# Adding the gather's z half from PSUM by VectorE, a full-height PSUM fill and a reordered last stage in a fused two-layer graph kernel

## The chip, the cores and the metric

One core of one Trainium2 chip. The metric is the device time of one launch in microseconds (us), the median of several runs. Executions of one kernel agree here to 0.1 to 0.2%. Ratios are formed only of kernels that ran in the same rounds on the same chip; where two experiments of different rounds are set side by side, the kernel before, which ran in all of them, differed by at most 0.6 us between the sets.

## The reference, cut to what matters

```python
# x (64, 256, 512), adj (64, 256, 256), nodemask all ones; float32
def layer0(x, adj, W):
    deg = sum(adj, -1)
    agg = adj @ x / max(deg, 1e-6)
    return relu(concat([x, agg], -1) @ W.T)          # 512 outputs
x = layernorm(x + layer0(x, adj, W))
def layer1(X, adj, mask, Wqk, Wv):
    q, k = split(X @ Wqk);  v = X @ Wv
    w = mask * rowsum(q * (adj @ (k * mask))) / sqrt(512)
    return softmax(w, axis=nodes)[..., None] * v
x = layernorm(x + layer1(x, adj, mask, Wqk, Wv))
```

The 64 graphs are worked on as 32 pairs, and layer 1 of one pair is interleaved with layer 0 of the next.

## The kernel before

All large products are done by a fast scheme with seven products in place of eight (named P1 to P7), some of them split once more. So the kernel is made of many matmuls of 256 or 512 columns into eight PSUM banks, with sums of blocks before and after them. TensorE runs without pause when everything is in time, and each bank is reused a few matmuls after it is read.

The part that the change is about is the product with adj of layer 0, the gather. Its bank `u` collects a running total over four steps (u1, u2, u3, u4), and after each step something reads it before the next step adds on:

```python
def gather(a, w, dst, u, p5, p2, own=None, rdeg=None, later=()):
    ...
        r12, r22 = dst[:, :, 0], dst[:, :, 1]              # the tile z, when own is given
    def onto(t, ps):                                       # own += bank * rdeg, first half of the columns
        for k in range(2):
            r = own[:, k, t, :HF]
            vec.scalar_tensor_tensor(r, ps[:, k * HF:(k + 1) * HF], rdeg[:, k, t:t + 1], r,
                                     op0=OP.mult, op1=OP.add)
    def u2():
        twice(u, "S2", "T2", start=False)
        act.copy(r12, of(u))                               # z from PSUM by ScalarE
        ...
    def u3():
        twice(u, "S3", "T3", start=False)
        act.copy(r22, of(u))
        vec.tensor_add(r22, of(p5), r22)
    def g3():
        twice(p5, "S4", "B22", start=False)
        vec.tensor_add(r12, of(p5), r12)
    def u4():
        twice(u, "A22", "T4", start=False)
        ...
# later, in norm0: own[second half] += z * rdeg, four VectorE instructions for a pair
```

VectorE, ScalarE, GpSimd and the DMA queue each have one queue, filled in the order in which the program issues to them. That order comes from a small model in the kernel: chains of steps (`queue`) are drained at `tick`, when the model thinks that an engine is free.

```python
def tick():
    while not quiet[0]:
        for c in list(chains):
            if c[2][0] <= clock[0] and c[3][0][0].free <= clock[0] + room[c[3][0][0]]:
                step(c)
                break
        else:
            return
```

The final scaling of layer 1 on ScalarE, with the output transfer behind it, is the chain "finish"; whatever is left of it is flushed where the next pair begins, ahead of the load of adj:

```python
for j in range(NP):
    ...
    flush("finish")                  # scale on ScalarE, then issue out
    ...
    if j > 0:
        load_adj(j)                  # 0.5 MB, issued behind the outputs
        sumsA[j] = adj_sums(j)       # sa: sums of adj's blocks on GpSimd
```

A split product is four steps; the third waits for ScalarE's copy of the second, since it overwrites that half bank:

```python
def second():
    mm(lo, s(1), b["T2"])
    act.copy(q[0][:, HF:], lo)
def third():
    mm(lo, s(2), b["T3"])
    ...
```

And the sums of x1's transposed blocks for layer 1 (`x1T_s` on VectorE, the first row's and S1's second-level sums `x1T_i` on GpSimd) run during the gather:

```python
queue(1, "sums", *outer_sums(Y, vec), (vec, lambda Y=Y: inner_sums(Y, gp, 1)))
```

## Time and profile before

| what | before |
|---|---|
| time, median of 3 runs | 1880.53 us (1880.49 to 1882.17) |
| TensorE busy | 1859.2 us, 99% |
| VectorE busy | 1511.1 us, 80% |
| ScalarE busy | 1309.1 us, 70% |
| TensorE stalls, whole span | 26.3 us |

The last row isn't on a page of the profile. I took each matmul's start from the trace, subtracted the start of the one before, and took off the time that the columns of the one before need at full pace (0.21 us for 256 columns of f32 or 512 of bf16, 0.43 us for 512 of f32); what is over 0.04 us counts as a stall. A product that runs at half pace at the start thus counts with half its time. All stalls in this document are computed so, from one profiled execution of each kernel.

Groups of instructions are shown by tile; the columns are count, then minimum, median and maximum in ns, first and last start, shapes.

```profile
L90 DVE TENSOR_TENSOR x1T_s<-x1T_s,x1T x32: 691/692/694, 89.1 to 1841.3; 128x512 f32<-128x512 f32 x32
```

```profile
L90 DVE TENSOR_TENSOR v<-v,fifth x62: 424/426/1017, 119.3 to 1835.1; 128x256 f32<-128x256 f32 x62
```

The addition to v is 0.43 us in most pairs and over 1 us at worst.

### The profile page before, as it was taken

The page shows a single profiled execution, that of the slowest core. Times are in us where ns is not written, and L with a number is a line of the kernel's source. Part 1 is how long each engine was busy: PE and PEld are TensorE (multiplying, and loading weights), DVE is VectorE, ACT ScalarE, POOL GpSimd, SP SyncE. Part 2 cuts the span into 40 slices and gives each one's busy share as a digit, 9 for nine tenths or more (in the row PEclk, how much of TensorE's full clock was granted, in tenths as well). Part 3 has the DMA queues.
Part 4 walks back from the last instruction along what each step waited for, and adds up shares of the span by engine and source line. Part 5 has one row for each costly group of instructions (what it writes and reads, how often), then busy time and mean ns, then how long its engine had stood idle before and what let it go on. Part 6 is the DMA issues. An engine that isn't in the chain of part 4 may idle for free.

```text
span 1878.8 us, 25005 instructions
## 1 busy us (share of the span) xinstructions
PE 1859.2 (99%) x7000; PEld 1314.0 (70%) x7000; DVE 1511.1 (80%) x3180; ACT 1309.1 (70%) x3274; POOL 909.2 (48%) x1251
## 2 busy tenths in 40 slices
PE   9999999999999999999999999999999999999997
PEld 5667777767777677677677777776776777776765
DVE  6787888778887778887778887788877788877887
ACT  3667776677777677767777766777676777767766
POOL 4455443555444554535554535554445544355532
PEclk9999999999999999999999999999999999999999
DMA  6123334333333433343333334333434233433321
GB/s 225 57 69 82 100 94 113 90 90 96 107 97 88 114 82 99 90 118 85 100 91 103 96 98 106 85 99 96 110 85 113 80 103 94 110 94 86 99 64 51
DMA packets 380714, 181.27 MB, mean 96 GB/s; under 512 B 263712, under 2 KB 345248, under 8 KB 380576
## 3 DMA queue, kind: packets, MB, share of 16 engines
q1 hardware_dynamic: 380576, 179.67, 35.4%
q8 instruction: 57, 0.93, 0.2%
q14 instruction: 81, 0.66, 0.1%
HBM read 114.10 MB, written 34.06 MB: 79 GB/s over the span
## 4 chain that ended last, share of the span: by engine, by line
PE 96%; DVE 2%; ACT 1%; DMA 0%; issue 0%; POOL 0%; DVEq 0%; ACTq 0%
PE bank L175 96%; ACT own L90 1%; DVE v L90 0%; DVE own L90 0%; ACT bank L90 0%; DVE turn L90 0%; DMA wqk<-wqk_t 0%; DVE tv L90 0%; DVE y L90 0%; PE bank L628 0%; POOL xT_s L90 0%; DVE bank L90 0%; POOL sa L90 0%; ACT x1T L90 0%; DVE st L90 0%
## 5 line engine op out<-in xcount | busy, mean ns | idle before, releaser
L90 ACT COPY bank<-bank 128x256 f32<-128x256 f32 (+1 forms) x768 | 332.3, 435 | 235.8 <-PE bank L175 224.7
L90 DVE TENSOR_TENSOR y<-bank,y 128x512 f32<-128x512 f32 x256 | 170.5, 686 | 131.9 <-ACT y L90 131.3
L90 ACT ACTIVATE own<-own,shift,rstd 128x512 f32<-128x512 f32 x255 | 199.8, 808 | 0.9 <-DVE shift L90 0.9
L175 PE MATMUL bank<-tv,sa 128*128 128x256 f32 x768 | 192.5, 380 | 1.0 <-DVE tv L90 0.9
L90 POOL TENSOR_TENSOR x1T_s<-x1T,x1T_s 128x256 f32<-128x256 f32 x64 | 63.6, 1013 | 267.7 <-PE bank L175 267.7
L90 POOL TENSOR_TENSOR x1T_i<-x1T_s 128x128 f32<-128x128 f32 x128 | 101.1, 790 | 182.8 <-DVE x1T_s L90 182.8
L90 ACT ACTIVATE junk<-own,less 128x512 bf16<-128x512 f32 x254 | 183.7, 723 | 3.0 <-DVE less L90 2.1
L175 PEld LDWEIGHTS bank<-tv,sa 128*128 128x128 f32 x768 | 145.4, 190 | 49.9 <-issue 23.1
L90 ACT COPY y<-bank 128x512 f32<-128x512 f32 x192 | 108.8, 583 | 95.2 <-PE bank L175 93.7
L90 POOL TENSOR_TENSOR sa<-adj 128x256 f32<-128x256 f32 x128 | 94.7, 740 | 165.9 <-DMA adj<-adj_t 152.1
L175 PE MATMUL bank<-w,x1T_s 128*128 128x512 f32 (+1 forms) x384 | 168.3, 521 | 0.0
L90 POOL TENSOR_TENSOR x1T_i<-x1T 128x256 f32<-128x256 f32 x64 | 55.4, 866 | 221.6 <-DMA x1T<-turn 209.0
L175 PE MATMUL bank<-t,xT_s 128*128 128x512 f32 (+1 forms) x384 | 159.3, 524 | 2.5 <-ACT own L90 1.5
L175 PE MATMUL bank<-t,x1T_s 128*128 128x512 f32 (+1 forms) x384 | 158.1, 521 | 0.3 <-ACT y L90 0.3
L90 DVE TENSOR_TENSOR v<-bank,v 128x512 f32<-128x512 f32 x186 | 119.2, 682 | 48.8 <-PE bank L175 48.8
L175 PE MATMUL bank<-w,xT_s 128*128 128x512 f32 (+1 forms) x384 | 153.1, 521 | 0.0
L175 PE MATMUL bank<-t_i,xT_i 128*128 128x256 f32 x512 | 152.7, 380 | 0.3 <-DVE own L90 0.2
L175 PE MATMUL bank<-t_i,x1T_i 128*128 128x256 f32 x512 | 152.2, 379 | 0.1
L175 PEld LDWEIGHTS bank<-t_i,x1T_i 128*128 128x128 f32 x512 | 97.1, 190 | 67.1 <-issue 48.6
L175 PEld LDWEIGHTS bank<-t_i,xT_i 128*128 128x128 f32 x512 | 94.6, 189 | 58.2 <-issue 45.7
L90 ACT COPY own<-bank 128x512 f32<-128x512 f32 x128 | 71.8, 587 | 89.9 <-PE bank L175 49.3
L175 PE MATMUL bank<-t,x1T 128*128 128x512 f32 x256 | 130.4, 592 | 0.0
(159 smaller groups left out, 4565.6 us busy)
## 6 DMA issues: line engine op xcount, KB each, us to landing
x<-x SPq DMA_DIRECT2D x64, 512.0 KB, 5.7
xT<-x_t SPq DMA_DIRECT2D x62, 512.0 KB, 5.5
out<-own SPq DMA_DIRECT2D x62, 512.0 KB, 3.2
x1T<-turn SPq DMA_DIRECT2D x480, 64.0 KB, 2.3
adj<-adj_t SPq DMA_DIRECT2D x64, 256.0 KB, 3.8
turn<-adj SPq DMA_DIRECT2D x64, 256.0 KB, 3.0
row<-d SPq DMA_DIRECT2D x31, 256.0 KB, 4.7
wqk<-wqk_t SPq DMA_DIRECT2D x4, 512.0 KB, 5.7
```

The costliest lines, as they stand in the source:

```text
L90: return self.tc.keep_in_program_order(getattr(self.engine, name)(out, *args, **kwargs))
L175: tc.keep_in_program_order(nc.tensor.matmul(ps, a, b, start=start, stop=True, skip_group_check=True))
```

## The change

The intent: z disappears as a tile. VectorE adds every block of the gather straight from PSUM to x1's buffer, `own`. The rest is small: the banks are filled at the start by ten products of full height (128 rows) instead of eight of one row, the first second-level sums are split so that the start can go earlier, GpSimd's sums of S1 are queued earlier, one transposition in the last pair goes earlier, and the last pair's order becomes "p p r p r p".

```diff
-        def onto(t, ps):
+        def onto(t, h, ps):
             for k in range(2):
-                r = own[:, k, t, :HF]
+                r = own[:, k, t, h * HF:(h + 1) * HF]
@@ u2, u3, g3 (u1, g2, u4 likewise)
             twice(u, "S2", "T2", start=False)
-            act.copy(r12, of(u))
+            if own is None:
+                act.copy(r12, of(u))
+            else:
+                onto(0, 1, u)
...
+                onto(1, 1, u)
+                onto(1, 1, p5)
...
+                onto(0, 1, p5)
@@ norm0
-                work += [(vec, lambda k=k, t=t: scaled(k, t)),
-                         (vec, lambda k=k, t=t, total=total: residual(k, t, total))]
+                work.append((vec, lambda k=k, t=t, total=total: residual(k, t, total)))
@@ fill
-    ones = const.tile([1, P], BF16, name="ones")
+    ones = const.tile([P, P], BF16, name="ones")
-               ones[:, None, :].to_broadcast([1, F // P, P]), start=True)
-    for pair in banks:
+               ones[:, None, :].to_broadcast([P, F // P, P]), start=True)
+    for pair in (banks[0], *banks):
@@ start and pairs
-    inner_sums(Xs[0], gp, 0)
-    inner_sums(Xs[0], gp, 1)
+    for part in (3, 1, 4):               # 3 and 4: the two halves of part 0
+        inner_sums(Xs[0], gp, part)
-            queue(1, "sums", *outer_sums(Y, vec), (vec, lambda Y=Y: inner_sums(Y, gp, 1)))
+            outer_Y = outer_sums(Y, vec)
+            queue(1, "sums", outer_Y[0], (vec, lambda Y=Y: inner_sums(Y, gp, 1)), *outer_Y[1:])
@@ last pair
+    turn_here(X, x1, 0, pf)
     run("l", l=open1)
     flush("norm", "mask")
-    turn_here(X, x1, 0, pf)
...
-    run("p p p r p r", p=p, r=r)
+    run("p p r p r p", p=p, r=r)
```

More of the change, by code (lines that the diff above doesn't have):

```diff
@@ L123, in resnorm_kernel @@
     banks = [[psum.tile([P, F], F32, name=f"bank{2 * n + k}") for k in range(2)] for n in range(4)]
-    (adjs, rows, xs, Xs, rdegs, sumsA, sumsM, owns, ys, zs, aggs, vs, x1Ts, scores, columns, rows_d, rows_w,
-     probs) = ({} for _ in range(18))
+    (adjs, rows, xs, Xs, rdegs, sumsA, sumsM, owns, ys, aggs, vs, x1Ts, scores, columns, rows_d, rows_w,
+     probs) = ({} for _ in range(17))
     clock, chains, shared, quiet = [0.0], [], [1.0], [False]
@@ L301, in inner_sums @@
         of_sum = lambda n: lambda k, e: X.s[:, k, X.slot[n]:X.slot[n] + 1, e]
-        ks, b = ((slice(0, 2), X.first_row), (slice(2, 3), of_sum(S1)), (slice(0, 1), of_sum(S4)))[part]
+        ks, b = ((slice(0, 2), X.first_row), (slice(2, 3), of_sum(S1)), (slice(0, 1), of_sum(S4)),
+                 *((slice(v, v + 1), lambda k, e, v=v: X.first_row(k, e)[:, v:v + 1]) for v in range(2)))[part]
         a11, a12, a21, a22 = (b(k, e) for k in range(2) for e in range(2))
@@ L411, in gather @@
             r11, r12, r21, r22 = (dst[:, :, t, h * HF:(h + 1) * HF] for t in range(NT) for h in range(2))
-        else:
-            r12, r22 = dst[:, :, 0], dst[:, :, 1]
-        def onto(t, ps):
+        def onto(t, h, ps):
             for k in range(2):
-                r = own[:, k, t, :HF]
+                r = own[:, k, t, h * HF:(h + 1) * HF]
                 vec.scalar_tensor_tensor(r, ps[:, k * HF:(k + 1) * HF], rdeg[:, k, t:t + 1], r,
@@ L432, in u1 @@
             else:
-                onto(0, u)
+                onto(0, 0, u)
             spare()
@@ L441, in g2 @@
             else:
-                onto(0, p2)
+                onto(0, 0, p2)
             spare()
@@ L457, in u3 @@
             twice(u, "S3", "T3", start=False)
-            act.copy(r22, of(u))
-            vec.tensor_add(r22, of(p5), r22)
+            if own is None:
+                act.copy(r22, of(u))
+                vec.tensor_add(r22, of(p5), r22)
+            else:
+                onto(1, 1, u)
+                onto(1, 1, p5)
             tick()
@@ L463, in g3 @@
             twice(p5, "S4", "B22", start=False)
-            vec.tensor_add(r12, of(p5), r12)
+            if own is None:
+                vec.tensor_add(r12, of(p5), r12)
+            else:
+                onto(0, 1, p5)
             tick()
@@ L471, in u4 @@
             else:
-                onto(1, u)
+                onto(1, 0, u)
             tick()
@@ L524, in norm0 @@
     def norm0(j):
-        own, z, rdeg = owns[j], zs.pop(j), rdegs.pop(j)
+        own = owns[j]
         x1Ts[j] = Side(pool, "x1T", S2)
         sq = []
-        def scaled(k, t):
-            o = own[:, k, t, HF:]
-            vec.scalar_tensor_tensor(o, z[:, k, t], rdeg[:, k, t:t + 1], o, op0=OP.mult, op1=OP.add)
         def residual(k, t, total):
@@ L832, in resnorm_kernel @@
             degrees(1)
-        zs[j] = pool.tile([P, 2, NT, HF], F32, name="z")
-        g = gather(sumsA.pop(j), T, zs[j], pw[1], y[1], y[0], owns[j], rdegs[j], T_late)
+        g = gather(sumsA.pop(j), T, None, pw[1], y[1], y[0], owns[j], rdegs.pop(j), T_late)
         def sums_next():
```

## The prediction

> **What bounds the kernel now.** I read the page first: the busy shares, then the chain that ended last.
>
> ```profile
> PE 1859.2 (99%) x7000; PEld 1314.0 (70%) x7000; DVE 1511.1 (80%) x3180; ACT 1309.1 (70%) x3274; POOL 909.2 (48%) x1251
> ...
> PE 96%; DVE 2%; ACT 1%; DMA 0%; issue 0%; POOL 0%; DVEq 0%; ACTq 0%
> ```
>
> TensorE is the bound, so work removed from VectorE or ScalarE is worth only the stalls of TensorE that it ends, and work that lands late before a matmul costs directly. How much there is to win: I laid the starts of the 7000 matmuls against the pace of an unstalled row (a 128x256 f32 record every 0.216 us, a 512-wide one every 0.429 us, read in the timeline). What is over that pace is about 26 us: 2.7 in the first weight products, some 8 from 21 to 100 us, 10.7 from 150 to 1796 us (0.2 in every pair, and 0.1 to 0.5 more in every second or third pair), 3 after 1820 us. After the last matmul (1867.0) 11.8 us more follow. The first look, at the start, is the timeline of TensorE and of its weight loads:
>
> ```profile
> 1.15 3.59 PE L175 MATMUL bank<-ones 1*128 1x512 bf16 x8 [1.15 <-DVE ones L90]
> 5.22 16.62 PE L175 MATMUL bank<-wqk 128*128 128x512 f32 x32 [0.47 <-DMA wqk<-wqk_t]
> ...
> 9.65 0.34 PEld L175 LDWEIGHTS bank<-wqk 128*128 128x128 f32 x1 [0.52 <-issue]
> 10.50 0.20 PEld L175 LDWEIGHTS bank<-wqk 128*128 128x128 f32 x1 [0.52 <-issue]
> 10.95 0.19 PEld L175 LDWEIGHTS bank<-wqk 128*128 128x128 f32 x1 [0.24 <-issue]
> ```
>
> Up to 10.5 us a product takes 0.85 us, after it 0.43: half clock for 5.3 us. The second look is where z costs, by tile:
>
> ```profile
> L90 DVE SCALAR_TENSOR_TENSOR own<-z,rdeg,own x128: 469/478/1023, 55.0 to 1819.2; 128x256 f32<-128x256 f32 x128
> L90 ACT COPY z<-bank x64: 574/585/586, 49.5 to 1805.8; 128x512 f32<-128x512 f32 x64
> L90 DVE TENSOR_TENSOR z<-bank,z x64: 691/692/693, 52.0 to 1808.7; 128x512 f32<-128x512 f32 x64
> ...
> L90 DVE SCALAR_TENSOR_TENSOR own<-bank,rdeg,own x192: 469/477/486, 45.9 to 1808.2; 128x256 f32<-128x256 f32 x192
> ```
>
> Third, the border between two pairs, in ScalarE's, the DMA queue's and TensorE's timelines (one pair of thirty that look alike):
>
> ```profile
> 797.01 1.50 ACT L90 ACTIVATE own<-own,shift,rstd 128x512 f32<-128x512 f32 x2
> 798.66 0.36 ACT L90 COPY bank<-bank 128x256 f32<-128x256 f32 x1 [0.15 <-PE bank L175]
> 799.95 0.36 ACT L90 COPY bank<-bank 128x256 f32<-128x256 f32 x1 [0.93 <-PE bank L175]
> ...
> 798.54 0.38 SPq L180 DMA_DIRECT2D out<-own  x1
> 799.03 1.34 SPq L180 DMA_DIRECT2D adj<-adj_t  x2
> ...
> 800.61 0.59 PE L175 MATMUL bank<-w,x1T_i 128*128 128x256 f32 x2
> ```
>
> The copy at 799.95 empties the half bank that the matmul at 800.61 overwrites; it ends 0.30 us before it. That is all the slack there is.
>
> **What the Trainium skill says.** "TensorE: Matmul & The Clock Gate", section "What's actually happening": the array starts at half clock, and a free-running window of 3.4 us of activity releases it. The trace agrees in kind: half pace to 10.5 us. It does not show whether one-row products count as activity. "SBUF — State Buffer", section "Who interferes with whom": a VectorE instruction with two SBUF inputs contends with GpSimd's reads, one with at most one SBUF input does not. The trace agrees: own<-z (two SBUF inputs) goes up to 1023 ns, own<-bank (one) never over 486. "Perfetto Trace Analysis", section "Optimizing Scalar/DVE Operations", gives VectorE a larger fixed cost on PSUM than on SBUF; here the two medians are 477 and 478 ns, so no difference shows.
>
> **The change, part by part.**
>
> z. Per pair it removes two ScalarE copies (2 x 0.585 = 1.17 us), two VectorE adds (2 x 0.692) and four scaled adds (4 x 0.604, the mean, = 77.3 us of the group over 128). It adds eight adds from PSUM of 0.436 to 0.477 us (83.8 us of the group over 192; the median). VectorE: minus 3.80, plus 3.5 to 3.8, so nothing; ScalarE: minus 1.17. None of it is on TensorE's path in the steady state: waits put down to z are 0.2 us in all. What matters is where VectorE's reads now stand, since TensorE reuses bank u. After u2 (its matmuls end at 772.61, the next on that bank starts 1.73 us later) VectorE has one sum of 0.69 ahead and then 0.87 for two reads: done at +1.56, just in time. After u3: 1.30 us to the next use, 0.2 for the result and 0.87 of reads, with two sums of 0.7 to 0.95 in the queue: 0 to 0.2 late, I say 0.05. Times 29 pairs: +1.5 us.
>
> What z's going moves. In the order of the built programs ScalarE's queue changes at the border of pairs: before, one half's final scaling stood early (778.7 and 780.2) and the other at 797.01; now both stand at the border, two before the copy of 798.66 and two between it and the copy of 799.95. Two scalings take 1.50. Then: 798.66 + 0.29 + 1.44 = 800.39 is when the second copy can start, it ends at 800.75, and a matmul starts 0.05 to 0.15 us after the copy that it waits for: 800.85 in place of 800.61. That is +0.24 us in each of 29 pairs: **+7.0 us**.
>
> The two output transfers now also stand together ahead of the next adj: it is issued after the second scaling, at about 801.0 in place of 799.03, behind 1 MB in place of 0.5, so the GpSimd sums of adj start at some 805.4 in place of 803.36. There they meet the two v additions with two SBUF inputs that lead, by turn, bank and own, to the first product of P6. Before, this collision is the one that makes the irregular stalls: 0.425 us for that addition and no stall, or 0.93 to 1.02 and a stall of 0.35 to 0.43. I count 3.8 us over 30 pairs now, 0.13 each, and expect 0.30 each: **+5 us** (from -4, if the sums come after both additions, to +12).
>
> Start. Ten full-height products (0.43 each, 1.15 to 5.4) join the weight products without the gap of 0.47, so the clock should come up at 5 to 8 us instead of 10.5: about 2.2 gained of the 2.7, less 0.2 for the longer fill. The smaller first sums on GpSimd let P1 start that early. But VectorE is 93 to 98% busy from 30 to 50 us, and there TensorE waits for it (0.90 for tv); and in the first gather its reads of z's banks stand behind those sums (up to +1). I keep **-1**.
>
> End. The transposes of the last pair fill the 0.4 us wait at 1831.5; a P4 product between P3's steps fills the 0.7 at 1862, but the last score then comes 0.43 later, so the softmax gains about 0.4. **-0.8**.
>
> Sum: +1.5 + 7.0 + 5 - 1 - 0.8 = +11.7, that is 1892. The two large terms rest on an order and on one pair's times, and all errors that I can think of (a shorter queue on ScalarE, now 1.17 us lighter) go the other way, so I take a third off: 1888.
>
> **The rivals.** (a) A small gain: start and end give 3 to 4 us and the steady state nothing, 1877. For it: VectorE's sum is even, ScalarE's falls, GpSimd is blocked less. Against it: the free 0.30 us before 800.61. (b) VectorE becomes the bound in the gather: reads behind other work stall u3 and u4 by 0.5 us each, +29 us, 1910. For it: VectorE is 80% busy and serves its queue in order; against it: the reads fit by the times above. (c) The late adj misses the v additions altogether: the 3.8 us go, and with the +7 the whole is about 1882.
>
> **Range and chances.** Rival (a) sets the low end, less a little: 1874; the upper ends of the collision term (+12) and of u3 (+5) the high one: 1902. 2% is 37.6 us. The whole sum of stalls that could be removed is 26 us, so faster by 2% is out of reach; slower by 2% takes rival (b) in full and more.
>
> **What would show it.** Right: in each pair a stall of about 0.2 us before the w,x1T_i matmul that follows two scalings and a copy on ScalarE; both output transfers next to each other, adj landing 2 us later against TensorE, the v additions near 0.8 us; wqk products at 0.43 us from before 8 us on; no z rows; own<-bank 448 times, never over 0.5 us. Wrong: those copies ending earlier, no regular stall, adj's sums clear of the v additions (then 1876 to 1882); or long waits of TensorE for own, in the gather (then over 1900).

## The result, and the profile after

| | before | after |
|---|---|---|
| time, median of 4 runs of the same rounds | 1881.35 us (1880.49 to 1882.70) | 1908.35 us (1908.26 to 1908.41) |
| ratio after / before | | 1.0143 (1.0125 to 1.0160) |
| TensorE busy | 1859.2 us | 1874.7 us |
| VectorE busy | 1511.1 us | 1499.5 us |
| ScalarE busy | 1309.1 us | 1277.5 us |

The kernel became 1.4% slower, 27 us. That is within 2%, as the prediction thought most likely, but outside its range (1874 to 1902).

The page of the changed kernel, its busy line and its chain by engine:

```profile
PE 1874.7 (98%) x7002; PEld 1306.7 (69%) x7002; DVE 1499.5 (79%) x3244; ACT 1277.5 (67%) x3210; POOL 896.9 (47%) x1255
...
PE 89%; DVE 6%; ACT 3%; issue 1%; DMA 1%; POOL 1%; SPq 0%; DVEq 0%; ACTq 0%
```

VectorE, ScalarE and GpSimd all have less to do than before, and still the chain that ends last goes through them for more of the span. So the loss is not work; it is the time at which work is done. Where TensorE stalls, from the trace (us; the number of times in brackets):

| stall, 150 to 1820 us | before | after | predicted addition | measured addition |
|---|---|---|---|---|
| third step of P3 in layer 1 (after ScalarE's copy) | 0 | 9.7 (29) | +7.0 | +9.7 |
| u4 of the gather (after VectorE's reads of u3) | 0 | 7.4 (27) | +1.5 for u2 and u3 | +7.4 |
| first product of P6 in layer 0 (after the v additions) | 4.9 (14) | 17.1 (25) | +5 | +12.2 |
| a step of P2 in layer 0 | 5.8 (29) | 5.8 (29) | 0 | 0 |
| all stalls before 150 us | 12.7 | 10.5 | -1 | -2.1 |
| all stalls after 1820 us | 3.0 | 3.2 | -0.8 | +0.3 |

In sum the stalls go from 26.3 to 54.0 us, 27.7 more, and the last matmul starts 27.8 us later (1866.99, then 1894.79). The account closes.

**u4.** VectorE's three x1T_s sums and GpSimd's first sum of them in one gather of the kernel before (start and duration in us):

```profile
772.75 0.68 DVE L90 TENSOR_TENSOR x1T_s<-x1T 128x512 f32<-128x512 f32 x1
773.47 0.69 DVE L90 TENSOR_TENSOR x1T_s<-x1T_s,x1T 128x512 f32<-128x512 f32 x1
774.08 0.94 DVE L90 TENSOR_TENSOR x1T_s<-x1T 128x512 f32<-128x512 f32 x1
...
773.51 0.96 POOL L90 TENSOR_TENSOR x1T_i<-x1T_s 128x128 f32<-128x128 f32 x1 [4.80 <-DVE x1T_s L90]
```

The three sums follow each other here, and only the third is lengthened, to 0.94 us. The timelines of VectorE, GpSimd and TensorE of the changed kernel in one gather:

```profile
374.05 0.68 DVE L90 TENSOR_TENSOR x1T_s<-x1T 128x512 f32<-128x512 f32 x1
374.65 0.87 DVE L90 SCALAR_TENSOR_TENSOR own<-bank,rdeg,own 128x256 f32<-128x256 f32 x2
375.44 0.91 DVE L90 TENSOR_TENSOR x1T_s<-x1T_s,x1T 128x512 f32<-128x512 f32 x1
376.27 0.94 DVE L90 TENSOR_TENSOR x1T_s<-x1T 128x512 f32<-128x512 f32 x1
377.13 1.65 DVE L90 SCALAR_TENSOR_TENSOR own<-bank,rdeg,own 128x256 f32<-128x256 f32 x4
...
375.76 0.90 POOL L90 TENSOR_TENSOR x1T_i<-x1T_s 128x128 f32<-128x128 f32 x1
376.62 0.90 POOL L90 TENSOR_TENSOR x1T_i<-x1T_s,x1T_i 128x128 f32<-128x128 f32 x1
...
378.05 1.13 PE L175 MATMUL bank<-tv,adj 128*128 128x256 f32 x4
```

The first `own<-bank` row is the two reads of u2. They now stand between the first and the second x1T_s sum, and this pushes the second sum into the time of GpSimd's own sums of the first (375.76 and 376.62). The second sum takes 0.91 us where it took 0.69; the third takes 0.94 as before. The reads of u3 start at 377.13; the first two of them are done near 378.0, and u4, at 378.05, waits for them.

**Third step.** ScalarE, the DMA queue and TensorE at the border of two pairs, in the changed kernel:

```profile
398.66 1.50 ACT L90 ACTIVATE own<-own,shift,rstd 128x512 f32<-128x512 f32 x2
400.32 0.36 ACT L90 COPY bank<-bank 128x256 f32<-128x256 f32 x1 [0.15 <-PE bank L175]
400.59 1.52 ACT L90 ACTIVATE own<-own,shift,rstd 128x512 f32<-128x512 f32 x2
402.01 0.37 ACT L90 COPY bank<-bank 128x256 f32<-128x256 f32 x1
...
400.19 2.32 SPq L180 DMA_DIRECT2D out<-own  x2
402.62 1.32 SPq L180 DMA_DIRECT2D adj<-adj_t  x2
...
402.52 0.67 PE L175 MATMUL bank<-w,x1T_i 128*128 128x256 f32 x2
```

Two scalings now stand between the two copies, and the second copy ends at 402.38 instead of with 0.30 us to spare. The matmul pair waits 0.255 us for it. It then shows 0.67 us where an unstalled pair shows 0.59: the second matmul loses 0.078 us more. Both outputs are issued ahead of adj.

**P6.** GpSimd, VectorE, ScalarE and TensorE later in the same pair:

```profile
406.96 0.73 POOL L90 TENSOR_TENSOR sa<-adj 128x256 f32<-128x256 f32 x1 [7.62 <-DMA adj<-adj_t]
407.76 0.80 POOL L90 TENSOR_TENSOR sa<-sa,adj 128x256 f32<-128x256 f32 x1
408.52 0.72 POOL L90 TENSOR_TENSOR sa<-adj 128x256 f32<-128x256 f32 x1
...
407.48 0.48 DVE L90 TENSOR_TENSOR v<-v,fifth 128x256 f32<-128x256 f32 x1
...
408.60 0.92 DVE L90 TENSOR_TENSOR v<-v,fifth 128x256 f32<-128x256 f32 x1
409.45 1.29 DVE L90 STREAM_TRANSPOSE turn<-own 128x512 f32<-128x512 f32 x2
410.67 1.39 DVE L90 TENSOR_TENSOR bank<-bank,fifth 128x256 f32<-128x256 f32 x4
...
411.10 1.07 ACT L90 COPY own<-bank 128x512 f32<-128x512 f32 x2 [1.63 <-DVE bank L90]
...
411.82 1.96 PE L175 MATMUL bank<-t,xT_s 128*128 128x512 f32 x4 [0.23 <-POOL sa L90]
```

adj came late, so GpSimd's sums of it reach over both additions to v: here the first takes 0.48 and the second 0.92 us, where an undisturbed one takes 0.43. The delay travels on: behind the additions VectorE has the transposition (turn) and the sums in bank, ScalarE's copies to own wait 1.63 us for those, and the first product of P6 overwrites the bank that the first of these copies reads: that copy ends at 411.68, P6 starts at 411.82. In the kernel before at most one of a pair's two additions is over 0.44 us (16 of 31 pairs); now both are in 22 of 31. The group over the whole run, by tile, moves its median from 426 to 904 ns:

```profile
L90 DVE TENSOR_TENSOR v<-v,fifth x62: 424/904/969, 117.3 to 1863.4; 128x256 f32<-128x256 f32 x62
```

The matmul's line names GpSimd's `sa` as the releaser. That is only the semaphore that came last by the profile: these sums aren't an operand of it, 18 of the 25 waits of this kind are put down to ScalarE's copy to own, and adj_early below, which takes away the collision, takes away this stall.

### The profile page after: what moved, and what is told of

Same layout as the page of the kernel before. It is cut to its first block, busy times and chain, and to the rows that moved or that the text cites. A ratio compares the mean times of both kernels' runs of the same rounds, so it can differ in the third digit from the quotient of the medians. Undisturbed runs are those within 1.5% of the kernel's fastest.

```text
span 1906.6 us, 24982 instructions
## 1 busy us (share of the span) xinstructions
PE 1874.7 (98%) x7002; PEld 1306.7 (69%) x7002; DVE 1499.5 (79%) x3244; ACT 1277.5 (67%) x3210; POOL 896.9 (47%) x1255
## 4 chain that ended last, share of the span: by engine, by line
PE 89%; DVE 6%; ACT 3%; issue 1%; DMA 1%; POOL 1%; SPq 0%; DVEq 0%; ACTq 0%
PE bank L175 89%; ACT own L90 2%; DVE v L90 2%; DVE own L90 1%; ACT bank L90 1%; DVE turn L90 1%; DMA w<-w_t 1%; DVE bank L90 0%; DVE t_i L90 0%; DVE t L90 0%; POOL xT_s L90 0%; DVE tv L90 0%; POOL sa L90 0%; DVE y L90 0%; SPq L180 0%
## 5 line engine op out<-in xcount | busy, mean ns | idle before, releaser
L90 DVE SCALAR_TENSOR_TENSOR own<-bank,rdeg,own 128x256 f32<-128x256 f32 x448 | 189.0, 472 | 12.5 <-PE bank L175 12.3
L90 POOL TENSOR_TENSOR x1T_s<-x1T,x1T_s 128x256 f32<-128x256 f32 x64 | 67.9, 1079 | 273.0 <-PE bank L175 273.0
L90 POOL TENSOR_TENSOR x1T_i<-x1T_s 128x128 f32<-128x128 f32 x128 | 88.0, 687 | 179.1 <-DVE x1T_s L90 179.1
L90 DVE TENSOR_TENSOR agg<-bank,agg 128x512 f32<-128x512 f32 x96 | 65.5, 683 | 125.9 <-ACT agg L90 124.7
```

What stands on the lines that cost most here:

```text
L90: return self.tc.keep_in_program_order(getattr(self.engine, name)(out, *args, **kwargs))
```

## The experiments

**The theory:** all three losses come from orders of queues that z's removal moved. (1) Both final scalings at the border delay ScalarE's copy: the third step. (2) adj behind two outputs lets GpSimd's sums block both v additions: P6. (3) The reads of u2 push the second x1T_s sum, too, under GpSimd's sums: u4. **Rivals:** A, the other parts of the change cost the time; B, VectorE is simply too full, or its reads from PSUM cost as such, so that moving queues gains little.

The results in one table; stalls in us from 150 to 1820 us, of one profiled run each. "u4" counts the wait before it and inside it. The profiled run isn't always a median one: that of finish_early took 1885.28 us, 1.9 below its median.

| kernel | time (us) | ratio to before | third step | u4 | P6 |
|---|---|---|---|---|---|
| before | 1881.35 | 1 | 0 | 0 | 4.9 |
| after | 1908.35 | 1.0143 | 9.7 | 7.4 | 17.1 |
| z_only | 1909.64 | 1.0148 | 9.7 | 6.7 | 15.7 |
| rest_only | 1879.35 | 0.9988 | 0 | 0 | 6.7 |
| adj_early | 1891.70 | 1.0055 | 9.7 | 7.4 | 0.2 |
| finish_early | 1887.13 | 1.0030 | 0 | 7.2 | 3.2 |
| gp_wait | 1907.37 | 1.0140 | 9.7 | 7.1 | 16.1 |
| gp_wait2 | 1899.44 | 1.0098 | 9.7 | 0 | 14.7 |
| s3_late | 1884.41 | 1.0015 | 0 | 3.1 | 5.4 |
| all3 | 1878.55 | 0.9986 | 0 | 3.0 | 0.5 |
| all4 | 1875.61 | 0.9971 | 0 | 0 | 0.6 |
| rest_adj | 1873.79 | 0.9959 | 0 | 0 | 0.3 |
| fill_only | 1879.73 | 0.9993 | 0 | 0 | 4.1 |
| row10 | 1881.92 | 1.0003 | 0 | 0 | 6.5 |

In the rows before and after the times are those of the result's own rounds. The kernel before measured 1880.94, 1881.48 and 1880.97 us in the three sets of rounds (first four experiments; gp_wait, s3_late, all3 and rest_adj; the last four). The 95% intervals of the ratios are about 0.0014 to either side. All experiments computed correct results.

**z_only.** The kernel before with only the z hunks (`gather`, `norm0`, no z tile).

> The kernel before with only the z part of the change. Theory (three losses by order of queues, all brought by z's going: third step of P3 9.7 us, first product of P6 12.2 us more, u4 7.4 us): about 1881 + 29 = 1910 us, with all three kinds of stall of the changed kernel in the profile. Rival A (the split of the inner sums and the new order of queues cost the time, z costs little): under 1895 us.

1909.64 us, with all three stalls. The whole loss belongs to z's removal. Its trace shows, in all pairs but the last, the order of the changed kernel on every engine: the earlier queueing of GpSimd's sums of S1 moved nothing there.

**rest_only.** The changed kernel without the z hunks.

> The changed kernel without its z part (fills of full height, split inner sums, earlier transposes, P3's order). Theory: none of the three stalls, so a little under before: 1878 to 1880 us (the start gave 1.95 us, the end nothing). Rival A: over 1886 us, with a part of the stalls.

1879.35 us, none of the new stalls: rival A falls. What it gains is 1.6 us by the medians, and its interval (0.9974 to 1.0002) just touches no gain.

**adj_early.** The changed kernel with adj's load issued ahead of P4 and P3. In the built programs only the DMA queue's order differs.

```diff
         if j > 0:
-            load_adj(j)
+            if j == 1:
+                load_adj(j)
@@ end of the pair
             b8()
+            if j + 1 < NP:
+                load_adj(j + 1)
             run("p l p l p l", p=p, l=open1)
```

> The changed kernel with adj's load issued before P4 and P3, thus ahead of both outputs. Theory (P6's stalls come from GpSimd's sums of a late adj that block both v additions): the v additions fall to about 0.45 us each, P6's stalls fall from 17.1 us to under 3, and the time from 1908.4 to about 1891 us; third step (9.7) and u4 (7.4) stay. Rival B (VectorE is late on its own, as a queue in order that now reads z from PSUM): the stalls of P6 stay above 10 us, time above 1902 us.

1891.70 us, as expected to within 1 us. By tile:

```profile
L90 DVE TENSOR_TENSOR v<-v,fifth x62: 424/425/427, 118.2 to 1847.1; 128x256 f32<-128x256 f32 x62
```

None of the 62 additions is over 427 ns now; P6's stalls are 0.2 us. The third step (9.7) and u4 (7.4) stay to the tenth, so they are separate causes, and VectorE has no general shortage at P6.

**finish_early.** The changed kernel with one half's chain "finish" drained early, as it was by chance of the order before.

```diff
                 b1(None)
                 run("g f", **g)
+                done = [c for c in chains if c[1] == "finish"][:1]
+                for c in done:
+                    while len(c[3]) > 1:
+                        step(c)
...
-            run("k h h" if j > 1 else "h h", k=k, h=h)
+            if j > 1:
+                run("k", k=k)
+                for c in done:
+                    step(c)
+            run("h h", h=h)
```

> The changed kernel with one half's final scaling and output put back to where it stood before (after u4 of the gather and after the next P2 step), the z part kept. Theory: the stall at the third step of P3 (9.7 us) goes, and with only one output ahead of adj P6 falls from 17.1 to about 5 us as in the kernel before; u4 (7.4 us) stays: about 1886.5 us. Rival B (VectorE's reads of z are the loss as such): third step goes at most, P6 and u4 stay: about 1898 us.

1887.13 us: the third step is gone, P6 is at 3.2 us with one output ahead of adj, u4 stays. This edit moves two queues at once (ScalarE's and the DMA queue's), and on VectorE one small instruction (shift) that goes with the scaling. adj_early has shown the DMA queue's part alone, with the third step untouched, so the third step's 9.7 us belong to ScalarE's order; shift was not tested apart.

**gp_wait.** To test why u4 is late: GpSimd's sums of S1 held back until VectorE has read u3.

```diff
-            queue(1, "sums", outer_Y[0], (vec, lambda Y=Y: inner_sums(Y, gp, 1)), *outer_Y[1:])
+            queue(1, "sums", *outer_Y)
...
-                run("c d j k e j", s=s, j=jj, k=k, **g)
+                run("c d j k e", s=s, j=jj, k=k, **g)
+                edge = small.tile([P, 1], F32, name="edge")
+                gp.tensor_add(edge, owns[j][:, 1, 1, 0:1], owns[j][:, 1, 1, 1:2])
+                inner_sums(Y, gp, 1)
+                run("j", j=jj)
```

> The changed kernel with GpSimd's sums of the S1 row of x1T held back until VectorE has read u3 (a tiny GpSimd add that reads the last block of own holds its queue). The orders on TensorE, VectorE and ScalarE are those of the changed kernel. Theory (these sums block VectorE's second and third x1T_s sums, 0.91 and 0.94 us instead of 0.69, and so u4): the sums fall to 0.69, the u4 stall (7.4 us) goes, time 1901 us. Rival (VectorE's queue of three sums and six reads is too long as such): u4's stall stays above 4 us, time above 1904 us.

1907.37 us, which looks like the rival. But the profile shows that the experiment failed: the tiny add ran at 372.26 and ended 3.6 us before the sums that it was to hold (376.07), and they collided as before. It read the half of own that isn't written by u3. This run says nothing on the question.

**gp_wait2.** The same with the right half.

```diff
-                gp.tensor_add(edge, owns[j][:, 1, 1, 0:1], owns[j][:, 1, 1, 1:2])
+                gp.tensor_add(edge, owns[j][:, 1, 1, HF:HF + 1], owns[j][:, 1, 1, HF + 1:HF + 2])
```

> gp_wait mended: there the tiny add read the half of own that is written before the gather, so it held nothing back; now it reads the half that VectorE writes from u3. Theory (GpSimd's sums of the S1 row block VectorE's second and third x1T_s sums, 0.91 and 0.94 us instead of 0.69, and so u4): the sums fall to 0.69, the u4 stall (7.4 us) goes, time about 1901 us. Rival (VectorE's queue of three sums and six reads is too long as such): u4's stall stays above 4 us, time above 1904 us.

1899.44 us, and u4's stall is gone, with the orders of TensorE, VectorE, ScalarE and the DMA queue those of the changed kernel. By tile:

```profile
L90 DVE TENSOR_TENSOR x1T_s<-x1T_s,x1T x32: 675/678/693, 87.7 to 1860.1; 128x512 f32<-128x512 f32 x32
```

The sum's median is 678 ns (909 in the changed kernel). So it is the collision with GpSimd that makes VectorE late; the length of its queue, with the same order, is not enough for a stall.

**s3_late.** Another way to help u4: the third x1T_s sum behind the reads of u3.

```diff
-... inner_sums(Y, gp, 1)), *outer_Y[1:])
+... inner_sums(Y, gp, 1)), outer_Y[1])
...
-                run("c d j k e j", s=s, j=jj, k=k, **g)
+                run("c d j k e", s=s, j=jj, k=k, **g)
+                queue(1, "sums", outer_Y[2])
+                run("j", j=jj)
```

> The changed kernel with the third x1T_s sum queued on VectorE behind the reads of u3; in the built program this also brings one half's final scaling and output back to their early place, as the loads' order is then that of the kernel before. Theory: all three kinds of stall go and P6 has about 5 us as before: 1879 to 1880 us, 7.4 below finish_early. Rival (the PSUM reads cost as such): not below 1885 us.

1884.41 us, between the theory (1879.5) and the rival (1885). The third step and P6 are as in the kernel before, since the move brought the early scaling back. But u4 still loses 3.1 us, most of it inside u4: the second sum (0.92 us, still under GpSimd's sums) and, newly, the inversion of the degrees stand ahead of the reads. The expectation treated u4's wait as gone with one sum, and that was too simple.

**all3.** s3_late, finish_early and adj_early together.

> All three repairs together: the third x1T_s sum behind the reads of u3, one half's final scaling early, adj's load before P4 and P3. Theory: no stalls of P6 at all, 1879.5 - 4.9 = 1874.5 us (1872 to 1877). Rival: with VectorE's reads of z from PSUM still there, not below 1880 us.

1878.55 us: P6 is clear; u4's 3.0 us are there as in s3_late. Below the rival's 1880, above the theory's 1874.5.

**all4.** all3, with the second x1T_s sum behind the reads of u3 too. Its time in the kernel's own model stays at the old place, so that no other engine's order moves.

```diff
+            def hold():
+                vec.free = max(vec.free, clock[0]) + shared[0] * (0.07 + 512 / 960)
-... inner_sums(Y, gp, 1)), outer_Y[1])
+... inner_sums(Y, gp, 1)), (vec, hold))
...
+                free = vec.free
+                outer_Y[1][1]()
+                vec.free = free
                 queue(1, "sums", outer_Y[2])
```

> all3 with the second x1T_s sum moved behind the reads of u3 as well; nothing else moves on any engine. Theory (what is left of u4's wait in all3, 2.8 us inside u4 and 0.2 before it, is VectorE's 0.92 us sum ahead of the reads of u3): both go, 1878.5 - 3.0 = 1875.5 us. Rival (VectorE is simply full there): the sum is missed elsewhere, by P1's last step or by P6 and P7 of the layer, and the time stays within 1 us of all3 or above.

1875.61 us against an expected 1875.5. VectorE's timeline in one gather of this kernel:

```profile
373.72 1.66 DVE L90 SCALAR_TENSOR_TENSOR own<-bank,rdeg,own 128x256 f32<-128x256 f32 x4 [0.58 <-PE bank L175]
375.30 0.68 DVE L90 TENSOR_TENSOR x1T_s<-x1T_s,x1T 128x512 f32<-128x512 f32 x1
```

VectorE waits 0.58 us for TensorE before the reads of u3: the direction of the wait has turned round. Every read of z from PSUM is still in this kernel, and the three new stalls are gone, so rival B falls. That it is faster than the kernel before is not z's merit: the early adj and the other parts alone give more, as the next run shows.

**rest_adj.** The changed kernel without the z part, with adj early: the same edit as in adj_early.

> The changed kernel without its z part, with adj's load before P4 and P3. Theory: P6's stalls (6.7 us in rest_only) go: 1872.5 us (1872 to 1875); the difference from all3 is what z's removal is worth once the queues are repaired: within 2 us of zero.

1873.79 us, the fastest of all and 0.4% under the kernel before. The second half of the expectation failed: all3, in the same rounds, is 4.8 us slower and not within 2, and 3.0 of these are u4's stall. all4, the repaired z, is 1.8 us above it, but the intervals (0.9946 to 0.9973, and 0.9958 to 0.9983) overlap and the two ran in different rounds: z's removal, repaired, is worth nothing or costs a little.

**fill_only** and **row10.** The kernel before with ten products of full height, or with ten of one row.

```diff
# both
-    for pair in banks:
+    for pair in (banks[0], *banks):
# fill_only alone
-    ones = const.tile([1, P], BF16, name="ones")
+    ones = const.tile([P, P], BF16, name="ones")
-               ones[:, None, :].to_broadcast([1, F // P, P]), start=True)
+               ones[:, None, :].to_broadcast([P, F // P, P]), start=True)
```

> The kernel before with only the fill changed: ten products of full height in place of eight of one row. Theory (full height counts as work for the clock, one row does not): full clock from about 4.3 us instead of 10.5, first xT_i product near 19 us instead of 21.7, about 1879 us (2 less).

> The kernel before with ten products of one row in place of eight. If full height is what brings the clock up: clock at about 10.5 us as before, time within 1 us of before or up to 0.5 more. Rival (the closed gap of 0.5 us before the weight products does it): clock up by 5 to 7 us and about 1879 us.

TensorE's timeline from 0 to 12 us, fill_only first:

```profile
1.17 4.45 PE L175 MATMUL bank<-ones 128*128 128x512 bf16 x10 [1.17 <-DVE ones L90]
5.55 6.74 PE L175 MATMUL bank<-wqk 128*128 128x512 f32 x14
```

```profile
1.16 4.44 PE L175 MATMUL bank<-ones 1*128 1x512 bf16 x10 [1.16 <-DVE ones L90]
5.53 7.05 PE L175 MATMUL bank<-wqk 128*128 128x512 f32 x9
```

The fill takes as long and the gap is closed in both, but by 12 us fill_only has begun 14 weight products and row10 nine. In fill_only the products are 0.43 us apart from the second on; in row10 the first six take 0.85 us or more. One trace each would be thin evidence, since the start differs from run to run. But all 11 profiles with full-height fills reach the full pace between 4 and 7 us, and all three with one-row fills (before, z_only, row10) between 10 and 11.5 us. So it is full height that brings the clock up early, not the closed gap. The expected 4.3 us was met in the changed kernel, whose last fills are 0.32 and 0.22 us apart, and not in fill_only, where all ten stay at 0.40 to 0.43 and the first weight product still takes 1.0 us. The first product with xT_i starts at 19.88 us (row10: 22.32, before: 21.70). The times, 1879.73 and 1881.92, agree with that, though the intervals of both reach no change.

## Why the prediction was wrong

**The direction and the mechanisms were right, the size was not:** forecast +7.5 us, measured +27. The 20 us between them are 7.2 us more of stalls than forecast at P6, 5.9 at u4 and 2.7 at the third step, and 4.2 us that were taken off the sum as "a third"; start and end err by 1.1 each and cancel. Point by point along the sum:

- **The bound.** Right: TensorE, and only stalls count. VectorE's busy time did not grow (1511.1 to 1499.5 us), the group `own<-bank` is 448 long and never over 485 ns.
- **The third step, +7.0.** Mechanism right, size 9.7. The delay of the copy was foreseen almost to the digit (0.24 forecast, 0.255 measured). The step that failed is the count of what one stall costs: each is followed by a second loss of 0.078 us in the same pair of matmuls, 2.3 us over 29 pairs.
- **The reads of u2 and u3, +1.5.** The failed step is "0 to 0.2 late, I say 0.05". It had the two sums "of 0.7 to 0.95" in the queue, and then chose nearly the best case. Measured: 0.14 to 0.22 us late in 27 of 29 pairs, plus 0.107 us of follow-up each, 7.4 us. The part that was missing is that u2's reads push the second sum under GpSimd's sums (0.69 to 0.91 us); gp_wait2 shows that without this the wait is zero.
- **The collision at P6, +5 (-4 to +12).** Mechanism right, adj_early shows it. The failed step is "0.30 each": it was 0.59 us a pair (17.1 over 29). The prediction took one collision of an addition as the unit, as before; with adj this late 47 of the 62 additions are lengthened, in 22 of 31 pairs both. Its reading of the kernel before was too coarse as well: it saw 0.425 us and no stall, or 0.93 to 1.02 and a stall of 0.35 to 0.43, but that trace also has additions of 0.47 to 0.85 us, and its 14 stalls run from 0.09 to 0.44 us.
- **The start, -1.** Measured -2.1 before 150 us. The clock came up even earlier than foreseen: the stalls up to 21.7 us fell by 2.8 us (5.1 to 2.3), where 2.0 net had been forecast. The loss set against it, up to 1 us, was 0.7 net from 21.7 to 150 us.
- **The end, -0.8.** Measured +0.3. The wait at 1831.5 (0.39 us before) was filled, but the earlier transposes wait 0.78 us themselves for the last normalisation; the P4 product removed the 0.7 us wait, and 0.35 us appeared before the last score's transposition. 11.8 us follow the last matmul in both kernels.
- **"I take a third off: 1888."** This went the wrong way. The reason given, that errors could only make it cheaper, was untrue for every one of the three terms. Rival (b) had the size (1910) but not the cause: it made VectorE the bound in the gather, with stalls of 0.5 us each at u3 and u4. u4's was 0.27 us and u3 showed none, and in all4, with the same reads, VectorE waits for TensorE.

Why the kernel's model places both scalings late without z was read from the built orders only; no run tested it. Nor is it settled whether repaired z is slower than no z change at all.

## What to carry to other kernels

TensorE had no slack here, and taking work off the others was worth nothing by itself. So first write down, for each buffer that the bound engine reuses, which instruction frees it, how long before, what stands ahead of it in its queue, and what another engine runs at the same time that lengthens it. If a removal shifts an in-order queue, compare the built orders of the two kernels and count every instruction that changed its neighbours, at its slow, collided duration; and add to each stall what the next instruction loses after it. Here the load that feeds GpSimd was best issued by when its sums run (P6 17.1 to 0.2 us in adj_early), and not by when its data are needed.

## What the Trainium skill lacked or had wrong

- "TensorE: Matmul & The Clock Gate", section "What's actually happening", speaks of activity but does not say that the height of the products counts. Ten one-row products over 4.4 us left the next six at 0.85 us or more; ten of 128 rows over the same time had the second one at 0.43.
- "SBUF — State Buffer", section "Who interferes with whom", has the rule right: two SBUF inputs collide (0.69 to 0.91 us, 0.43 to 0.92), one SBUF input beside PSUM does not (485 ns at most over 448). It says that issue order decides who blocks, and gives no size for this pair of operations. Here both sides lose in the same stretch: GpSimd's 128x128 sums take 0.90 us in place of 0.46 while VectorE's two sums take 0.91 and 0.94.
- No page that I read gives the cost that follows a stall: the second matmul of a pair that had waited lost a further 0.078 us, or 0.107 us at u4.
